# One-hot edge products that read `pre` rows in place: 64-row single-pass products, two blocks at once, in a graph network kernel

## The chip, the cores and the metric

The kernel runs on one core of one Trainium2 chip. The metric is the device time of one execution in microseconds (us), the median of several runs. TensorE (PE) multiplies matrices and writes PSUM, VectorE (DVE) and ScalarE (ACT) work on elements, GpSimd (POOL) issues the indirect transfers here, and SyncE (SP) the plain ones. PEld is TensorE's loading of the stationary operand.

## What is computed

64 graphs of 256 nodes with 256 features pass through four layers. One adjacency matrix `adj` (256 x 256, few entries besides the diagonal) serves all graphs. Layers 0, 1 and 3 are edge networks, layer 2 is an attention.

```python
def edge_layer(h_t, A_a, A_m, W1, b1, W2, b2, Wa, ba, Wm, bm, beta1, beta2, beta3):
    pre_u = jnp.einsum('bud,dk->buk', h_t, W1[:d])
    pre_v = jnp.einsum('bvd,dk->bvk', h_t, W1[d:])
    hidden = jax.nn.relu(pre_u[:, :, None, :] + pre_v[:, None, :, :] + b1)
    S = jax.nn.sigmoid(jnp.einsum('buvk,ko->buvo', hidden, W2)[..., 0] + b2[0])
    a_t = jnp.einsum('buv,bud->bvd', S * A_a, h_t)
    m_t = jnp.einsum('uv,bud->bvd', A_m, h_t) * h_t
    return beta1 * h_t + beta2 * (a_t @ Wa + ba) + beta3 * (m_t @ Wm + bm)
```

The attention layer makes features, a softmax over all pairs plus `adj`, and adds the weighted features to its input. `S` is multiplied by `adj`, so a score is only needed where `adj` is not zero: per edge (u, v), the sum of row u of `pre_u` and row v of `pre_v`, a relu and a weighted sum over 256 numbers.

## The kernel before, in words

The adjacency matrix is cut into 16 blocks of 64 source nodes by 64 target nodes, named (k, m, i): sources 64 k to 64 k + 63 of half m (128 nodes), targets 64 i to 64 i + 63. `edges()` (L529), run once, numbers the edges of each block, at most 128 to a block; what is over goes to a list of rest edges (`left`), and the diagonal is treated apart (`own`, L757). For each block it writes a one-hot matrix `pick` (edge of the block by 64 sources and 64 targets), its transpose for spreading scores back (`gu`, `gva`), and for fetched blocks the node numbers `ids_u`, `ids_v`.

Graphs go in pairs (g = 0, 1, side by side in the last dimension, so a row has 512 numbers). Two such pairs are in work at a time, sides "a" and "b". While the scores of one side's layer are taken (`scores`, L700: "heavy"), the other side's next steps run between them (`after` L880, `attention` L425, `before` L646: "light"); `beside` (L911) interleaves them by counts that each light step yields (`STEPS` L45, `beside` L656). Below, one such interleaving is a stage; a period is six stages, and there are 16 periods, 96 stages. Every engine then works through its instructions in order.

- `before` (L646) makes `pu` and `pv` (pre_u and pre_v + b1) for half m and graph g: a product on PE, a copy on ACT, an addition on DVE. When a half is complete, both go as tables to DRAM (L677, SP's queue), and `fetch` (L814) starts the first six indirect transfers (POOL). `rows_u` and `rows_v` (L833, L841) copy rows on ACT into `pre`, where each made block has a 128-row operand: its 64 u rows and its 64 v rows. The last step, `mixed` (L334), multiplies `adj` into h.
- `scores` (L700) gets the edge sums of 16 blocks in two ways. Made blocks (`made`, L764): one fp32 product of 128 rows, `pick` by `pre`, into a PSUM buffer `ga` (L768); further rows of `pre` are copied as it goes (L773). Fetched blocks (`got`, L783): an indirect transfer of table u's rows, then one of table v's rows that adds (`compute_op`, L829). Rest edges take two such transfers as well. Each sum of a block and graph is rated by one DVE instruction (`rated`, L716), relu times `w2row` with an accumulated sum.
- `rated_all` (L740), for m = 0 and m = 1, takes the tanh (`val`) and multiplies `gva` by it into `rm`, four DVE products each. `spread` (L865) puts `rm` back to source rows by one-hot products with `gu`; `early` (L849) does the rest edges (`guo` by `ro`, products of 64 rows) and the diagonal.

Eight blocks are made and eight fetched, but in two of six stages (`more`, L642: side "a" in the last layer, side "b" in the second edge layer, the stages with attention beside them) six are made and ten fetched. In these two stages graph 1's part of `mixed` is put among the made blocks (L781).

The constants that set this, and the made product:

```python
FAST = [(k, 0, i) for k in range(2) for i in (2, 3)] + [(0, 1, i) for i in range(4)]
FETCHED = [(k, 0, i) for k in range(2) for i in (0, 1)] + [(1, 1, i) for i in range(4)]
MORE = FAST[6:]
FETCHES = [(0, 0), (1, 0), (2, 0), (0, 1), (3, 0), (1, 1)]
FETCHES += [(-1, 0), (2, 1), (4, 0), (3, 1), (-1, 1), (5, 0), (6, 0), (4, 1), (7, 0), (5, 1), (6, 1), (7, 1)]
AHEAD = 6
...
mm(out=t, lhsT=pick[:, k, 4 * m + i, :], rhs=pre[:, n], start=True, stop=True)
```

In `FETCHES`, (f, x) is block f's transfer from table u (x = 0) or v (x = 1), and f = -1 the rest edges. [...]

Of the kernel before, what the change touches and what calls it, by code (L numbers as in the profile page):

```python
# [9 lines left out]
FP = mybir.dt.float32  # L10
I32 = mybir.dt.int32
AF = mybir.ActivationFunctionType
ALU = mybir.AluOpType
# [19 lines left out]
FAST = [(k, 0, i) for k in range(2) for i in (2, 3)] + [(0, 1, i) for i in range(4)]  # L33
FETCHED = [(k, 0, i) for k in range(2) for i in (0, 1)] + [(1, 1, i) for i in range(4)]

MORE = FAST[6:]
FIRST = 4

FETCHES = [(0, 0), (1, 0), (2, 0), (0, 1), (3, 0), (1, 1)]
FETCHES += [(-1, 0), (2, 1), (4, 0), (3, 1), (-1, 1), (5, 0), (6, 0), (4, 1), (7, 0), (5, 1), (6, 1), (7, 1)]  # L40
FETCHES_MORE = FETCHES[:-2] + [(8, 0), (6, 1), (9, 0), (7, 1), (8, 1), (9, 1)]
# [60 lines left out]
def adj_seq_kernel(ctx: ExitStack, tc: tile.TileContext, a: dict, out: bass.AP):  # L102
# [18 lines left out]
    def behind(engine):  # L121

        return tc.issue_after(engine.last.ins)

# [158 lines left out]
    def open_pools(stack):  # L283
        pool = lambda name, bufs, **k: stack.enter_context(tc.tile_pool(name=name, bufs=bufs, **k))
        k = dict(fm=pool("fm", 2), wk=pool("wk", 2), one=pool("one", 1))
        k["ps"] = pool("ps", 5, space=bass.MemoryType.PSUM)
        k["ga"] = pool("ga", 3, space=bass.MemoryType.PSUM)
        return k

    def stages(pools):  # L290
# [211 lines left out]
    def few(stack):  # L502
# [10 lines left out]
        gva = one.tile([P, 2, 8, 64], FP, name="gva")  # L513
# [4 lines left out]
        ids_u = one.tile([P, len(FETCHED + MORE)], I32, name="ids_u")  # L518
        ids_v = one.tile([P, len(FETCHED + MORE)], I32, name="ids_v")
# [9 lines left out]
        def edges():  # L529
            scratch = Scratch(*(  # L530
                (one.tile([P, n * 2 * D], FP, tag=tag + "b", name="scratch"), n * 2 * D)
                for tag, n in (("pre", len(FAST)), ("fetched", FIRST))
# [15 lines left out]
            for m in range(2):  # L548
# [6 lines left out]
                for k in range(2):  # L555
# [3 lines left out]
                    )  # L559

# [31 lines left out]
            for k, m in ((0, 0), (1, 0), (1, 1), (0, 1)):  # L592
# [11 lines left out]
                    vector.scalar_tensor_tensor(gva[:, k, ms, :], gv, 0.5, w, ALU.mult, ALU.mult)  # L604
                    here = [b for b in FETCHED + MORE if b[:2] == (k, m)]
                    if here:
                        i, n = here[0][2], len(here)
                        f = (FETCHED + MORE).index(here[0])
                        for b, x, ids in ((P * m + 64 * k, gu[:, k, ms, :], ids_u), (None, gv, ids_v)):
# [6 lines left out]
                            o = ids[:, f : f + n]  # L616
                            if b is None:
                                vector.tensor_tensor(o, r[:, i : i + n], v0[:, i : i + n], ALU.add)
                            else:
                                vector.tensor_scalar(o, r[:, i : i + n], float(b), None, ALU.add)  # L620
# [21 lines left out]
        def more(st, l):  # L642

            return (st["side"], l) in (("a", LAST), ("b", GNN[1]))

        def before(st, l):  # L646
# [4 lines left out]
            pre = one.tile([P, len(FAST), 2 * D], FP, tag="pre" + st["side"], name="pre")  # L651
# [10 lines left out]
            st["pu"], st["pv"], st["pre"] = pu, pv, pre  # L662
# [4 lines left out]
            for m, g in order:  # L667
# [7 lines left out]
                if g == 1:  # L675
                    for rows, x in zip(st["tables"], (pu, pv)):
                        nc.sync.dma_start(out=rows[blk(m)], in_=flat(x)[:, m])  # L677
                    if m == 0:
                        st["fetches"] = list(FETCHES_MORE if more(st, l) else FETCHES)
# [18 lines left out]
            yield from mixed(st, l, later if past else None, (0,) if more(st, l) else (0, 1))  # L698

        def scores(st, l, placed):  # L700
# [8 lines left out]
            pre = st["pre"]  # L709
# [20 lines left out]
            blocks, fast = (FETCHED + MORE, FAST[:6]) if more(st, l) else (FETCHED, FAST)  # L730
            t = one.tile([P, len(FETCHED + MORE) - FIRST, 2, D], FP, tag="fetched", name="fetched")
            st["fetched"] += [t[:, f] for f in range(len(blocks) - FIRST)]
            fetched = st["fetched"]
            fetch(st, len(FETCHES_MORE))
# [5 lines left out]
            def rated_all(cols, m):  # L740
# [22 lines left out]

            def made():  # L764
                for n, (k, m, i) in enumerate(fast):
                    t = ga.tile([P, 2, D], FP, tag="ga", name="ga")
                    with stay(tensor):
                        mm(out=t, lhsT=pick[:, k, 4 * m + i, :], rhs=pre[:, n], start=True, stop=True)  # L768
                    tile_scores(t, k, m, i)
                    if 2 * n + 2 < len(fast):  # L770

                        with tc.issue_after(past[-1]) if past else nullcontext(), tc.issue_after(st["rows"]):
                            rows_u(st, 2 * n + 2, 2, *FAST[2 * n + 2][:2])  # L773
                            if n != 1:
                                rows_v(st, 2 * n + 2, 2, FAST[2 * n + 2][0])
# [4 lines left out]
                    if n == 2 and more(st, l):  # L780
                        yield from mixed(st, l, None, (1,), ga)  # L781

            def got(made):  # L783
                for f, block in enumerate(blocks):
# [47 lines left out]

        def rows_u(st, f, n, k, m):  # L833

            h = halves[k]
            scalar.copy(
                st["pre"][h, f : f + n],
                st["pu"][h, m].rearrange("p g d -> p (g d)").unsqueeze(1).to_broadcast([64, n, 2 * D]),
            )

        def rows_v(st, f, n, k):  # L841

            for n in range(f, f + n):
                i = FAST[n][2]
                scalar.copy(
                    st["pre"][halves[1 - k], n], st["pv"][halves[i % 2], i // 2].rearrange("p g d -> p (g d)")
                )
# [200 lines left out]
```

## Time and profile before

| what | value |
|---|---|
| median of 3 runs | 3455.84 us (3452.6 to 3463.16) |
| span of the profiled execution, first to last instruction | 3442.3 us (its whole time is not listed) |
| mean granted TensorE clock | 0.990 |
| instructions | 48323 |
| indirect transfers, table u / table v | 832 / 832, and 96 / 96 for the rest edges |
| indirect transfers of the queue q0 | 461.49 MB, 65.2% of the DMA engines' time |

The page gives for each engine its busy time and its share of the span; since matmuls overlap in the array, PE's busy share says only that PE has work. A group line names the operation, what it writes and reads, shapes and count, then busy time in all, the mean ns of one, and the engine's idle time before these instructions with what ended it. An fp32 product appears as two records. A few such lines, in that form:

```profile
L827 POOL DMA_INDIRECT fetched<-tablev,ids_v x832 | 1324.7, 1592 | 353.1 <-issue 249.4
L827 POOL DMA_INDIRECT fetched<-tableu,ids_u x832 | 840.9, 1011 | 544.3 <-DMA tableu<-pu 283.9
L79 DVE SCALAR_TENSOR_TENSOR junk<-fetched,L_gnn_w2row 128x256 f32<-128x256 f32 x1664 | 643.6, 420 | 219.9 <-DMA fetched<-tablev,ids_v 218.3
L79 PE MATMUL ps<-L_gnn_w,hT 128*128 128x512 f32 x1536 | 708.1, 598 | 6.1 <-DMA hT<-in_xT_dram 6.1
```

The first two are POOL's indirect transfers, whose 0.98 to 1.6 us are the time POOL spends on issuing one; the third is the rating of fetched blocks, with 218.3 us in which DVE stood for a landing. L79 is the helper that records every instruction of PE, DVE and ACT, so groups are told apart by tiles.

### The profile page before, as it was taken

Reading aid. Unit: us, or ns where it says so; the run is one execution under the profiler, and the core shown is the slowest. Engines: PE = TensorE matmul, PEld = TensorE weight load, DVE = VectorE, ACT = ScalarE, POOL = GpSimd, SP = SyncE. Lnnn points to the kernel's source line nnn. Section 1 sums busy time; section 2 is a strip of 40 time slices with the busy share of each in tenths; the row PEclk is TensorE's granted clock in tenths of the full one; section 3 lists DMA queues with packets and bytes.
Section 4 is the critical chain, followed back from the end, with each engine's and each line's share of the span. In section 5 each row is a group of like instructions: output and inputs, shape, how many; then the busy total and the mean of one; then the engine's idle time right before and its main releaser. Section 6 shows DMA issues by size and latency. Waiting matters only on the chain.

```text
span 3442.3 us, 48323 instructions
## 1 busy us (share of the span) xinstructions
PE 3349.5 (97%) x14200; PEld 2071.0 (60%) x14200; DVE 2650.7 (77%) x10523; ACT 1556.4 (45%) x2833; POOL 2420.7 (70%) x1882
## 2 busy tenths in 40 slices
PE   6999999999999999999999999999999999999998
PEld 3566565666656566565665656656565665656665
DVE  4777787877877777777777878778787787777776
ACT  2444444444444444544444444444444444444452
POOL 3767777777776767677777776777767776776765
PEclk7999999999999999999999999999999999999999
DMA  5778787887878778787787877878787787787875
GB/s 146 161 181 194 167 200 169 192 184 175 202 168 196 174 180 194 170 195 182 184 184 172 198 173 188 186 167 206 169 194 175 177 199 171 191 177 182 192 169 128
DMA packets 289070, 620.81 MB, mean 180 GB/s; under 512 B 39072, under 2 KB 56352, under 8 KB 288800
## 3 DMA queue, kind: packets, MB, share of 16 engines
q0 software_dynamic: 204800, 461.49, 65.2%
q1 hardware_dynamic: 82416, 154.96, 12.9%
q8 instruction: 115, 1.88, 0.2%
q10 hardware_dynamic: 1584, 1.20, 0.1%
q14 instruction: 155, 1.27, 0.1%
HBM read 500.06 MB, written 117.44 MB: 179 GB/s over the span
## 4 chain that ended last, share of the span: by engine, by line
PE 67%; POOL 11%; DMA 9%; issue 7%; DVE 3%; ACT 2%; ACTq 0%; POOLq 0%; DVEq 0%; SPq 0%
PE ps L79 52%; PE ga L79 15%; POOL fetched L827 10%; DMA fetched<-tablev,ids_v 6%; DVE junk L79 1%; DMA tableu<-pu 1%; POOL left L827 1%; ACT pre L79 1%; DMA fetched<-tableu,ids_u 1%; DVE rm L79 1%; ACT val L79 1%; ACT pu L79 0%; DMA h<-in_x_dram 0%; DMA left<-tablev,left_v 0%; DMA hT<-in_xT_dram 0%
## 5 line engine op out<-in xcount | busy, mean ns | idle before, releaser
L827 POOL DMA_INDIRECT fetched<-tablev,ids_v x832 | 1324.7, 1592 | 353.1 <-issue 249.4
L827 POOL DMA_INDIRECT fetched<-tableu,ids_u x832 | 840.9, 1011 | 544.3 <-DMA tableu<-pu 283.9
L79 DVE SCALAR_TENSOR_TENSOR junk<-fetched,L_gnn_w2row 128x256 f32<-128x256 f32 x1664 | 643.6, 420 | 219.9 <-DMA fetched<-tablev,ids_v 218.3
L79 PE MATMUL ga<-pre,pick 128*128 128x512 f32 x1408 | 728.2, 611 | 24.8 <-ACT pre L79 13.5
L79 PE MATMUL ps<-L_gnn_w,hT 128*128 128x512 f32 x1536 | 708.1, 598 | 6.1 <-DMA hT<-in_xT_dram 6.1
L79 DVE SCALAR_TENSOR_TENSOR junk<-ga,L_gnn_w2row 128x256 f32<-128x256 f32 x1408 | 536.8, 419 | 124.0 <-PE ga L79 121.4
L79 PEld LDWEIGHTS ps<-L_gnn_w,hT 128*128 128x128 f32 x1536 | 280.3, 191 | 324.5 <-issue 294.2
L79 ACT COPY pre<-pv 64x512 f32<-64x512 f32 x704 | 434.2, 617 | 68.1 <-DVE pv L79 56.7
L79 ACT COPY pre<-pu 64x1024 f32<-64x1024 f32 x352 | 361.5, 1044 | 6.6
L79 PE MATMUL ps<-sa,h 128*128 128x256 f32 x1536 | 359.4, 380 | 0.0
L79 PEld LDWEIGHTS ps<-sa,h 128*128 128x128 f32 x1536 | 292.9, 191 | 108.3 <-issue 60.6
L79 ACT COPY pu<-ps 128x256 f32<-128x256 f32 x384 | 143.0, 372 | 470.8 <-PE ps L79 467.8
L79 PEld LDWEIGHTS ga<-pre,pick 128*128 128x128 f32 x1408 | 250.5, 192 | 170.1 <-issue 103.2
L79 DVE TENSOR_TENSOR rm<-gva,val 128x256 f32<-128x256 f32 x768 | 277.7, 420 | 60.8 <-ACT val L79 58.7
L79 PE MATMUL ps<-adj,h 128*128 128x256 f32 x1280 | 293.9, 381 | 3.4 <-issue 3.4
L79 PEld LDWEIGHTS ps<-adj,h 128*128 128x128 f32 x1280 | 244.1, 191 | 78.0 <-issue 41.4
L79 ACT ACTIVATE hb<-hT,L_gnn_zbias,scas 128x512 f32<-128x512 f32 x128 | 97.3, 806 | 414.5 <-DVE hT L79 391.1
L79 PEld LDWEIGHTS ps<-rm,gu 128*64 128x64 f32 x3072 | 176.2, 138 | 131.9 <-issue 70.8
L79 ACT COPY aT<-ps 128x512 f32<-128x512 f32 x192 | 112.5, 586 | 302.6 <-PE ps L79 302.6
L79 PE MATMUL ps<-rm,gu 128*64 128x128 f32 x3072 | 213.8, 281 | 35.5 <-DVE rm L79 35.5
L79 DVE TENSOR_TENSOR pv<-ps,L_gnn_b1row 128x256 f32<-128x256 f32 x384 | 161.9, 422 | 110.2 <-ACT pu L79 101.4
L79 PE MATMUL ps<-mT,L_gnn_Wm 128*128 128x512 f32 x512 | 240.6, 592 | 0.0
(149 smaller groups left out, 4213.1 us busy)
## 6 DMA issues: line engine op xcount, KB each, us to landing
tableu<-pu SPq DMA_DIRECT2D x192, 256.0 KB, 3.8
tablev<-pv SPq DMA_DIRECT2D x192, 256.0 KB, 2.7
hT<-in_xT_dram SPq DMA_DIRECT2D x32, 512.0 KB, 5.1
h<-in_x_dram SPq DMA_DIRECT2D x64, 256.0 KB, 4.8
out_dram<-h SPq DMA_DIRECT2D x64, 256.0 KB, 4.1
fetched<-tableu,ids_u POOLq DMA_INDIRECT x832, 3.8
fetched<-tablev,ids_v POOLq DMA_INDIRECT x832, 5.1
L_gnn_w<-in_L_gnn_W_dram SPq DMA_DIRECT2D x6, 256.0 KB, 4.8
```

The costliest lines, as they stand in the source:

```text
L79: self.last = getattr(self.engine, op)(*a, **k)
L827: this = nc.gpsimd.indirect_dma_start(out=to, out_offset=None, in_=rows, in_offset=bass.IndirectOffsetOnAxis(ap=ids, axis=0), compute_op=( ...
```

## The change

- `pick` by `pre` is replaced. `pre`, `rows_u` and `rows_v` are gone. `pu` and `pv` of each half are split into a high part in the type float32r (a copy on ACT) and the rest (a subtraction on DVE), and the products read these `parts` where they lie. One-hot matrices in float32r, `pick_u` and `pick_v`, are copied once in `edges()`.
- Made blocks come in pairs, k = 0 and k = 1, whose source rows and target rows lie in the same 64 partitions each. A pair is eight products of 64 rows (v rest, u rest, u high, v high; for each, k = 1 and k = 0), into two `ga` buffers, issued one behind another. `FAST` and `FETCHED` are chosen anew for that.
- All stages have 8 made and 8 fetched blocks; `more`, `MORE` and `FETCHES_MORE` are gone, and `mixed` is whole again at the end of `before`.
- Blocks 4 and 5 of the fetched are read from table v first, and u is added (`V_FIRST`); a transfer reads only half 0's table where it can.
- `rm` is one product of 128x1024 for each m, with `gva` and `rm` laid out anew.
- PSUM: four buffers for `ps` and four for `ga`.

```diff
-FAST = [(k, 0, i) for k in range(2) for i in (2, 3)] + [(0, 1, i) for i in range(4)]
-FETCHED = [(k, 0, i) for k in range(2) for i in (0, 1)] + [(1, 1, i) for i in range(4)]
-
-MORE = FAST[6:]
+FAST = [(k, m, 2 * j + k) for m in range(2) for j in range(2) for k in range(2)]
+FETCHED = [(k, m, 2 * j + 1 - k) for m in range(2) for j in range(2) for k in range(2)]
+
 FIRST = 4
+
+
+V_FIRST = (4, 5)
 
 FETCHES = [(0, 0), (1, 0), (2, 0), (0, 1), (3, 0), (1, 1)]
 FETCHES += [(-1, 0), (2, 1), (4, 0), (3, 1), (-1, 1), (5, 0), (6, 0), (4, 1), (7, 0), (5, 1), (6, 1), (7, 1)]
-FETCHES_MORE = FETCHES[:-2] + [(8, 0), (6, 1), (9, 0), (7, 1), (8, 1), (9, 1)]
...
+    def soon():
+
+        return tc.high_priority(offset=1000)
...
-        k["ps"] = pool("ps", 5, space=bass.MemoryType.PSUM)
-        k["ga"] = pool("ga", 3, space=bass.MemoryType.PSUM)
+        k["ps"] = pool("ps", 4, space=bass.MemoryType.PSUM)
+        k["ga"] = pool("ga", 4, space=bass.MemoryType.PSUM)
...
-        def mixed(st, l, later=None, graphs=(0, 1), buffers=None):
-
-            if 0 in graphs:
-                st["mT"] = one.tile([P, 2, 2, N], FP, tag="mT" + st["side"], name="mT")
-            mT = st["mT"]
-            for g in graphs:
-                t = buffers.tile([P, 2, 256], FP, tag="ga", name="ga") if buffers else psum()
-                for m in range(2):
-                    if buffers and m == 1:
-                        yield
-                    for c in range(2):
-                        mm(out=t[:, m, :], lhsT=st["h"][g][:, c, blk(m)], rhs=adj[:, c, :], start=c == 0, stop=c == 1)
+        def mixed(st, l, later=None):
+
+            st["mT"] = mT = one.tile([P, 2, 2, N], FP, tag="mT" + st["side"], name="mT")
+            for g in range(2):
+                t = psum()
+                product(t, st["h"][g], adj)
...
-        gva = one.tile([P, 2, 8, 64], FP, name="gva")
+        gva = one.tile([P, 2, 2, 4, 64], FP, name="gva")
+
+
+        pick_u = one.tile([P, 2, 2, P], FR, name="pick_u")
+        pick_v = one.tile([P, 2, 2, P], FR, name="pick_v")
...
+                for k, h in enumerate(halves):
+                    mine = slice(4 * m + k, 4 * m + k + 3, 2)
+                    scalar.copy(pick_u[h, m], pick[h, k, mine, :])
+                    scalar.copy(pick_v[h, m], pick[halves[1 - k], k, mine, :])
...
-            pre = one.tile([P, len(FAST), 2 * D], FP, tag="pre" + st["side"], name="pre")
+            parts = {
+                x: [one.tile([P, 2, 2 * D], FR, tag=x + y + st["side"], name=x + y) for y in "hl"] for x in "uv"
+            }
...
-                    if m == 0:
-                        rows_u(st, 0, 2, 0, 0)
-                    rows_v(st, 4 - 4 * m, 2, 0)
-                    st["rows"] = scalar.last.ins
+
+                    for x, (high, low) in ((pu, parts["u"]), (pv, parts["v"])):
+                        scalar.copy(high[:, m], flat(x)[:, m])
+                        vector.tensor_tensor(low[:, m], flat(x)[:, m], high[:, m], ALU.subtract)
...
-            yield from mixed(st, l, later if past else None, (0,) if more(st, l) else (0, 1))
+            yield from mixed(st, l, later if past else None)
...
-                for g in range(2):
-                    for k in range(2):
-                        ms = slice(4 * m, 4 * m + 4)
-                        i = BLOCKS + 16 * m + 8 * g + 4 * k
-                        vector.tensor_tensor(
-                            rm[:, k, ms, g, :], gva[:, k, ms, :],
-                            val[:, i : i + 4].unsqueeze(2).to_broadcast([P, 4, 64]), ALU.mult
-                        )
+                of = slice(BLOCKS + 16 * m, BLOCKS + 16 * m + 16)
+                vector.tensor_tensor(
+                    rm[:, m], gva[:, m].rearrange("p k i v -> p (k i) v").unsqueeze(2).to_broadcast([P, 8, 2, 64]),
+                    val[:, of].rearrange("p (g x) -> p x g", g=2).unsqueeze(3).to_broadcast([P, 8, 2, 64]), ALU.mult
+                )
...
+            def sums(m, j):
+
+
+                both_ = [ga.tile([P, 2, D], FP, tag="ga", name="ga") for _ in halves]
+                order = [(pick_v, "v", 1, j), (pick_u, "u", 1, m), (pick_u, "u", 0, m), (pick_v, "v", 0, j)]
+                for n, (pick_, x, part, block) in enumerate(order):
+                    for k in (1, 0):
+                        h, first = halves[k], (n, k) == (0, 1)
+                        with stay(tensor) if first else behind(tensor), nullcontext() if first else soon():
+                            mm(out=both_[k], lhsT=pick_[h, m, j, :], rhs=st["parts"][x][part][h, block],
+                               start=n == 0, stop=n == 3)
+                return both_
+
             def made():
-                for n, (k, m, i) in enumerate(fast):
-                    t = ga.tile([P, 2, D], FP, tag="ga", name="ga")
-                    with stay(tensor):
-                        mm(out=t, lhsT=pick[:, k, 4 * m + i, :], rhs=pre[:, n], start=True, stop=True)
-                    tile_scores(t, k, m, i)
-                    if 2 * n + 2 < len(fast):
-
-                        with tc.issue_after(past[-1]) if past else nullcontext(), tc.issue_after(st["rows"]):
-                            rows_u(st, 2 * n + 2, 2, *FAST[2 * n + 2][:2])
-                            if n != 1:
-                                rows_v(st, 2 * n + 2, 2, FAST[2 * n + 2][0])
+                for n, (k, m, i) in enumerate(FAST):
+                    if k == 0:
+                        pair = sums(m, i // 2)
+                    tile_scores(pair[k], k, m, i)
                     if n in (1, 2) and not diagonal_later:
                         itself(n - 1)
                     count.append(n)
                     yield
-                    if n == 2 and more(st, l):
-                        yield from mixed(st, l, None, (1,), ga)
...
-                rows = st["tables"][x]
+                y = 1 - x if f in V_FIRST else x
+                rows, ids = st["tables"][y], (ids_u, ids_v)[y]
                 if f < 0:
                     to, ids = st["left"], (left_u, left_v)[x]
                     rows = rows.rearrange("n (g d) -> (n g) d", g=2)
                 else:
-                    to, ids = st["fetched"][f].rearrange("p g d -> p (g d)"), (ids_u, ids_v)[x][:, f : f + 1]
-                    if f < FIRST:
+                    k, m, i = FETCHED[f]
+                    to, ids = st["fetched"][f].rearrange("p g d -> p (g d)"), ids[:, f : f + 1]
+                    if (m, i // 2)[y] == 0:
                         rows = rows[blk(0)]
...
```

More of the change, by code (lines that the diff above doesn't have):

```diff
@@ L10 @@
 FP = mybir.dt.float32
+FR = mybir.dt.float32r
 I32 = mybir.dt.int32
@@ L517, in few @@
         gvo = one.tile([P, N], FP, name="gvo")
-        ids_u = one.tile([P, len(FETCHED + MORE)], I32, name="ids_u")
-        ids_v = one.tile([P, len(FETCHED + MORE)], I32, name="ids_v")
+        ids_u = one.tile([P, len(FETCHED)], I32, name="ids_u")
+        ids_v = one.tile([P, len(FETCHED)], I32, name="ids_v")
         left_u = one.tile([P, 1], I32, name="left_u")
@@ L530, in edges @@
             scratch = Scratch(*(
-                (one.tile([P, n * 2 * D], FP, tag=tag + "b", name="scratch"), n * 2 * D)
-                for tag, n in (("pre", len(FAST)), ("fetched", FIRST))
+                (one.tile([P, n * 2 * D], FP, tag=tag, name="scratch"), n * 2 * D)
+                for tag, n in (("fetchedb", FIRST), ("fetched", len(FETCHED) - FIRST))
             ))
@@ L603, in edges @@
                     scalar.copy(gv, t[:, :, halves[1 - k]])
-                    vector.scalar_tensor_tensor(gva[:, k, ms, :], gv, 0.5, w, ALU.mult, ALU.mult)
-                    here = [b for b in FETCHED + MORE if b[:2] == (k, m)]
+                    vector.scalar_tensor_tensor(gva[:, m, k], gv, 0.5, w, ALU.mult, ALU.mult)
+                    here = [b for b in FETCHED if b[:2] == (k, m)]
                     if here:
-                        i, n = here[0][2], len(here)
-                        f = (FETCHED + MORE).index(here[0])
+                        i = slice(here[0][2], here[0][2] + 3, 2)
+                        f = FETCHED.index(here[0])
+                        f = slice(f, f + 3, 2)
                         for b, x, ids in ((P * m + 64 * k, gu[:, k, ms, :], ids_u), (None, gv, ids_v)):
@@ L615, in edges @@
                             vector.tensor_reduce(r, y, AX.X, ALU.add)
-                            o = ids[:, f : f + n]
+                            o = ids[:, f]
                             if b is None:
-                                vector.tensor_tensor(o, r[:, i : i + n], v0[:, i : i + n], ALU.add)
+                                vector.tensor_tensor(o, r[:, i], v0[:, i], ALU.add)
                             else:
-                                vector.tensor_scalar(o, r[:, i : i + n], float(b), None, ALU.add)
+                                vector.tensor_scalar(o, r[:, i], float(b), None, ALU.add)
             t = psum().rearrange("p a (b e) -> p (a b) e", e=P)
@@ L640, in few @@
         flat = lambda t: t.rearrange("p m g d -> p m (g d)")
-        def more(st, l):
-            return (st["side"], l) in (("a", LAST), ("b", GNN[1]))
         def before(st, l):
@@ L660, in before @@
             ]
-            st["pu"], st["pv"], st["pre"] = pu, pv, pre
+            st["pu"], st["pv"], st["parts"] = pu, pv, parts
             if l != GNN[1]:
@@ L678, in before @@
                     if m == 0:
-                        st["fetches"] = list(FETCHES_MORE if more(st, l) else FETCHES)
+                        st["fetches"] = list(FETCHES)
                         if numbered:
@@ L708, in scores @@
             diagonal_later = placed and (st["side"], l) in (("b", GNN[0]), ("a", GNN[1]))
-            pre = st["pre"]
             raw = wk.tile([P, LATE.stop], FP, tag="raw", name="raw")
@@ L729, in scores @@
             st["left"] = left = one.tile([P, D], FP, tag="left", name="left")
-            blocks, fast = (FETCHED + MORE, FAST[:6]) if more(st, l) else (FETCHED, FAST)
-            t = one.tile([P, len(FETCHED + MORE) - FIRST, 2, D], FP, tag="fetched", name="fetched")
-            st["fetched"] += [t[:, f] for f in range(len(blocks) - FIRST)]
+            t = one.tile([P, len(FETCHED) - FIRST, 2, D], FP, tag="fetched", name="fetched")
+            st["fetched"] += [t[:, f] for f in range(len(FETCHED) - FIRST)]
             fetched = st["fetched"]
-            fetch(st, len(FETCHES_MORE))
+            fetch(st, len(FETCHES))
             def tile_scores(t, k, m, i):
@@ L779, in made @@
                     yield
-                    if n == 2 and more(st, l):
-                        yield from mixed(st, l, None, (1,), ga)
             def got(made):
-                for f, block in enumerate(blocks):
+                for f, block in enumerate(FETCHED):
                     if f == FIRST:
@@ L831, in fetch @@
                 fetches.append(this.ins)
[L833 to L847, printed above, removed]
         def early(st):
@@ L871, in spread @@
                     for k, h in enumerate(halves):
-                        mm(out=t[h, :, quarter(i)], lhsT=gu[:, k, 4 * m + i, :], rhs=rm[:, k, 4 * m + i],
+                        mm(out=t[h, :, quarter(i)], lhsT=gu[:, k, 4 * m + i, :], rhs=rm[:, m, 4 * k + i],
                            start=True, stop=True)
```

## The prediction

> **What bounds the kernel now.** I read the page's busy rows first, then the chain that ended last, then the groups by form, then windows over one period, then the timelines of PE and POOL. All durations are of the one profiled execution, whose span is 3442.3 us; the page gives no other time of it. The median of the runs is 3455.84, so about 13.5 us lie around the span; I add that to every span below.
>
> ```profile
> PE 3349.5 (97%) x14200; PEld 2071.0 (60%) x14200; DVE 2650.7 (77%) x10523; ACT 1556.4 (45%) x2833; POOL 2420.7 (70%) x1882
> ...
> PE 67%; POOL 11%; DMA 9%; issue 7%; DVE 3%; ACT 2%; ACTq 0%; POOLq 0%; DVEq 0%; SPq 0%
> ```
>
> PE is the first bound, but not alone: some 27% of the chain is POOL, DMA landing and "issue", the fetches. Next, what one period of six stages costs (a stage is one layer's scores of one side beside the other side's light steps; its end is the second tanh on `val`). Columns: length, then busy time of PE, PEld, DVE, ACT, POOL.
>
> ```profile
> 1421.42:1460.58 39.16, 38.28 (x162) 23.84 (x158) 30.98 (x123) 18.28 (x37) 26.89 (x22) 1.00 0.77 167
> 1460.58:1501.37 40.79, 40.40 (x178) 25.10 (x177) 32.71 (x128) 17.96 (x37) 28.62 (x23) 1.00 0.81 187
> 1501.37:1534.93 33.56, 33.56 (x148) 22.29 (x146) 26.86 (x106) 14.38 (x26) 25.94 (x21) 1.00 0.89 215
> 1534.93:1565.53 30.60, 30.00 (x133) 19.99 (x133) 24.51 (x100) 14.77 (x26) 23.06 (x18) 1.00 0.86 202
> 1565.53:1596.79 31.26, 31.26 (x128) 17.90 (x127) 23.18 (x96) 15.72 (x27) 22.07 (x17) 1.00 0.75 163
> 1596.79:1628.50 31.71, 31.71 (x128) 17.71 (x126) 25.21 (x100) 15.75 (x28) 21.77 (x17) 1.00 0.78 178
> ```
>
> Stages 1 and 2 carry the attention and 6 made / 10 fetched blocks; 3 to 6 have 8 / 8. The POOL column hides its load: between two transfers it has 0.30 us of "issue". The POOL timeline:
>
> ```profile
> 1558.59 1.54 POOL L827 DMA_INDIRECT fetched<-tablev,ids_v  x1 [0.30 <-issue]
> 1560.44 0.99 POOL L827 DMA_INDIRECT fetched<-tableu,ids_u  x1 [0.30 <-issue]
> ...
> 1594.32 0.98 POOL L827 DMA_INDIRECT fetched<-tableu,ids_u  x1 [4.05 <-DMA tableu<-pu]
> ```
>
> An 8-fetch stage issues 18 transfers: 9 x (0.98 + 0.30) + 9 x (1.55 + 0.30) = 28.2 us, of 30.6 to 33.6. So stages 3 to 6 have two bounds close together: PE, and the loop table write, 18 fetches, last landing (about 5.4 us), rating, `val`, `rm`, the other side's light steps, next table write.
>
> **The change part by part.** Groups that it removes or grows, and how TensorE treats 64-row products:
>
> ```profile
> L79 PE MATMUL ga<-pre,pick 128*128 128x512 f32 x1408 | 728.2, 611 | 24.8 <-ACT pre L79 13.5
> L79 ACT COPY pre<-pv 64x512 f32<-64x512 f32 x704 | 434.2, 617 | 68.1 <-DVE pv L79 56.7
> L79 ACT COPY pre<-pu 64x1024 f32<-64x1024 f32 x352 | 361.5, 1044 | 6.6
> L79 DVE TENSOR_TENSOR rm<-gva,val 128x256 f32<-128x256 f32 x768 | 277.7, 420 | 60.8 <-ACT val L79 58.7
> ```
>
> ```profile
> 1524.25 1.02 PE L79 MATMUL ga<-pre,pick 128*128 128x512 f32 x2
> 1525.20 1.13 PE L79 MATMUL ps<-ro,guo 64*128 64x256 f32 x8
> 1526.27 1.12 PE L79 MATMUL ga<-pre,pick 128*128 128x512 f32 x2
> 1527.23 3.17 PE L79 MATMUL ps<-L_gnn_w,hT 128*128 128x512 f32 x7
> ```
>
> *PE, removed.* A made product is two records; among others of its kind they start 0.86 us apart in all (0.43 each for 512 columns). There are 1408/2 = 704: 704 x 0.862 = 607 us.
>
> *PE, added.* 96 stages x 4 pairs = 384 pairs, each eight single-record products of 64 rows and 512 columns. Two prices are needed.
>
> First, one pass. No row shows a reduced-precision product. [...]
>
> Second, two row halves at once. The row of `ro,guo` shows it: eight records of 64x256, each 0.2135 of stream, start to next start in 1526.27 - 1525.20 = 1.07 us, where one after another would be 1.71. So halves overlap. [...] I take 1.25, since that group is the same shape of work with the same neighbours. The eight weight loads are inside that price (the `ro,guo` group hides eight too).
> 384 x 1.25 = 480: PE saves 607 - 480 = 127 us, 1.9 us in each 8-made stage (6.9 to 5.0), 0.17 in stages 1 and 2 (5.17 to 5.0; they now make 8). [...]
>
> *ACT.* Removed 704 x 0.617 + 352 x 1.044 = 802 us. Added: 384 copies of 128x512, nearest the 64x512 row: 384 x 0.617 = 237. ACT is no bound; what counts is that `pu` of the second half has 2 x 0.62 us before it, not 1.04 + 1.24, so its table goes out up to 1 us sooner, and that PE's waits for `pre` (13.5 on PE, 31.0 on weight loads) end. Of that 44.5 I count 20 as path.
>
> *DVE.* Added: 384 subtractions 128x512; the SBUF-only `own<-pu,pv` of that shape takes 689 ns: 265 us. The four `rm` products of a stage half (1.43 us together in the timeline) become one of 128x1024 (1.21, the setup's row of that shape): 192 x 0.22 = 42 less. Net +222, 2.3 us a stage: 2873 busy. Hidden while DVE's 5 to 8 us of waiting per stage is for PE and DMA; if that cover is gone it is +222. Behind the subtractions of half 0 in DVE's queue stand `pv` of half 1 (1.4 us later) and so `tablev`, for which POOL's eighth transfer waits; the seven before it (some 10 us) cover that.
>
> *POOL and DMA queue.* 64 blocks fewer: 64 x (1.59 + 1.01 + 0.60) = 205 us, all in stages 1 and 2, where PE leads: worth nothing by itself. Stages 3 to 6 keep 18 transfers and 28.2 us. The v-first order of two blocks and whole-table reads of two others stay behind transfers that wait for the same tables: nothing. SP's queue is unchanged.
>
> *Moved.* Graph 1's mix (8 records x 0.2135 = 1.72 us PE, one multiply on DVE) leaves the score steps of stages 1 and 2 for the end of the light steps one stage earlier: stage 2 loses 1.72 us before its table write, stage 6 gains 1.72 behind it, stage 1 both. No DMA is in it.
>
> *PSUM, new waits.* Four `ps` buffers for five: 0 to 1 us a stage (weight loads of `ps` wait for DVE's `junk` 30.9 us in all today); I take 0 for the sum. PE's products now wait for the rest parts from DVE; they are made before the last scores and the mix (3.4 us of PE) of the stage before: hidden; uncovered 0.62 + 0.69 = 1.3 us a stage, 126 in all. Queued behind PE's wait would be everything on PE. Setup: eight small copies, +3.
>
> *Sum.* By PE alone a period saves 4 x 1.9 + 2 x 0.17 = 7.9 us. By the loop: stage 2's table is 1.9 sooner (0.17 + 1.72); stages 3 and 4 are then one unbroken run of POOL (1500.91 to 1560.1), so they stay at -1.9; stage 5's light steps, with about 1.6 us less PE before the table write, make stage 6 end 3.5 sooner; stage 1 adds 0.17. So 3.7 against 7.9, and the smaller wins: 16 x 3.7 = 60. With 20 for `pre` and 3 for the setup: 3442 - 60 - 20 + 3 = 3365, and 13.5 around it: **3378 us**, 3340 to 3420 by itself. What is late next is POOL's queue.
>
> **Rivals.** *PE's full saving* (0.15): the loop has more slack than I count (stage 5's last landing was near 1594, its `val` at 1596.8). 3442 - 127 - 20 + 3 + 13.5 = 3312. [...] For: chain 67% PE. Against: 27% of it is fetches.
>
> *DVE takes over* (0.17, slower): DVE works in order, and its ratings of fetched blocks already hold it 218 us for landings. If the subtractions between `pv` of half 0 and of half 1 push the evacuations that the light steps need (`hT`, `pv`, `sa`), tables go out later, landings too, and DVE stands longer in front of them. All 222 us on the path and PE's 127 + 20 won: 3456 + 222 - 147 = 3531. It decides from where DVE's busy share of stages 3 to 6 passes about 0.93. Against: now 0.74 to 0.80, and 2.3 us makes it 0.82 to 0.9.
>
> *The products don't stream as said* (0.13, slower): 2.11 a pair, +203 - 20: about 3640. For: no row shows them. Against: `ro,guo`.
>
> *The fetch loop holds everything* (0.07): stages 3 to 6 keep their length, stages 1 and 2 win under 0.5 us: within 0.3%, 3450.
>
> **How the numbers follow.** Forecast 0.48. About 0.3% (10 us) is what a measurement of this kernel can tell from no change. Faster: 0.48 and 0.15, less 0.03 for a forecast eaten by the `ps` buffers: 0.60. Same: 0.07 and 0.01: 0.08. Slower: 0.17, 0.13 and 0.02: 0.32. The range takes in the PE rival nearly to its floor and the DVE rival: 3250 to 3535; it leaves out the product rival and the floor's tail.
>
> **What would show it.** PE: a group of eight 64*128 records of 64x512, start to next start near 1.25 us; 0.9 or 2.1 would be the ends. ACT near 990 us, DVE near 2870, POOL near 2250. Stages 3 and 4 should show POOL without waits for `tableu`, and PE with gaps for `rm` or `sa`. Wrong if PE's share stays at 97% with a shorter span (rival one), or if waits of PE for DVE grow to 100 us or more (rival two).

## The result, and the profile after

The changed kernel took **3585.86 us** (median of 4, 3577.73 to 3588.51) against 3454.98 before (4 runs): a ratio of 1.0372, 95% interval 1.0348 to 1.0397. It is 131 us slower; the forecast was 78 faster. The time lies above the range.

The page's busy row and chain (the chain was followed only a few per cent back, so it says nothing here):

```profile
PE 3286.3 (92%) x15864; PEld 2102.0 (59%) x15864; DVE 2827.9 (79%) x10331; ACT 995.2 (28%) x2169; POOL 2304.3 (64%) x1754
...
PE 4%; DVE 1%; DMA 1%; POOL 0%; ACT 0%; issue 0%; POOLq 0%; DVEq 0%; ACTq 0%
```

The span is 3576.0. PE is busy 63.2 us less, and idle 289.7 instead of 92.8: the span grew by 196.9 - 63.2 = 133.7. The mean granted clock fell from 0.990 to 0.969, which is 0.031 x 3576 - 0.010 x 3442 = 76 us of full clock, partly within PE's idle time. So PE's work shrank by 63 to 140 us (predicted: 127), and PE now stands idle.

One period, cut like that of the prediction (the same six stages, second tanh to second tanh; PE, PEld, DVE, ACT, POOL, clock):

```profile
1478.67:1512.16 33.49, 29.37 (x135) 19.14 (x132) 25.85 (x106) 10.70 (x25) 19.92 (x15) 0.90 0.64 121
1512.16:1561.13 48.97, 46.04 (x212) 28.79 (x212) 36.18 (x130) 14.92 (x34) 23.04 (x18) 0.97 0.59 140
1561.13:1602.11 40.98, 39.00 (x206) 26.30 (x202) 34.12 (x116) 9.74 (x22) 28.05 (x21) 1.00 0.78 195
1602.11:1634.63 32.52, 30.34 (x152) 21.22 (x152) 26.45 (x98) 8.13 (x18) 25.09 (x18) 0.95 0.84 189
1634.63:1666.78 32.15, 29.95 (x140) 17.58 (x142) 24.89 (x94) 9.09 (x20) 24.58 (x18) 1.00 0.77 174
1666.78:1699.35 32.57, 30.35 (x152) 17.85 (x148) 27.49 (x99) 8.99 (x19) 25.06 (x19) 1.00 0.81 177
```

In each of these stages PE is idle 2 to 4 us in all; in those of the prediction it was 0 to 0.9. A stage's tanh no longer falls at the same point of the attention, so I use another cut below: from one write of table u's second half to the next. By it the six stages of a period, A to F, take on the mean, in us (14 periods; the attention runs beside E and F):

| kernel | A | B | C | D | E | F | sum |
|---|---|---|---|---|---|---|---|
| before | 30.0 | 33.5 | 31.7 | 31.7 | 41.9 | 40.8 | 209.7 |
| after | 29.2 | 34.4 | 31.8 | 33.2 | 45.5 | 43.8 | 217.9 |

16 x 8.2 = 131: the loss is there every period, and 6.6 of the 8.2 lie in E and F (stages 1 and 2 of the prediction, by this cut). There PE is busy on the mean as long as before (41.3 and 40.5 us; before 41.7 and 40.0), but idle 4.2 and 3.4 us instead of 0.2 and 0.8. Of this idle time, 3.3 and 2.0 us are waits for `logits` and `e` from ACT, the steps of the softmax.

The groups that answer to those shown of before, first PE's `rm` group of before for comparison, then PE's made products (start, length):

```profile
L79 PE MATMUL ps<-rm,gu 128*64 128x128 f32 x3072 | 213.8, 281 | 35.5 <-DVE rm L79 35.5
```

```profile
L81 DVE TENSOR_TENSOR rm<-gva,val 128x1024 f32<-128x1024 f32 x192 | 234.9, 1224 | 54.1 <-ACT val L81 54.1
L81 DVE TENSOR_TENSOR ul<-pu,uh 128x512 fp32r<-128x512 f32 x192 | 132.0, 687 | 5.8 <-ACT uh L81 5.5
L81 DVE TENSOR_TENSOR vl<-pv,vh 128x512 fp32r<-128x512 f32 x192 | 131.4, 685 | 0.4
L81 PE MATMUL ps<-rm,gu 128*64 128x128 f32 x3072 | 213.7, 287 | 103.6 <-DVE rm L81 103.1
L835 POOL DMA_INDIRECT fetched<-tableu,ids_u x768 | 926.2, 1206 | 790.6 <-DMA tableu<-pu 553.7 <-issue 211.0 <-DVE ids_u L81 15.6
```

```profile
1524.04 0.49 PE L81 MATMUL ga<-vl,pick_v 64*128 64x512 f32 x2
1524.38 0.39 PE L81 MATMUL ga<-ul,pick_u 64*128 64x512 f32 x2
1524.60 0.40 PE L81 MATMUL ga<-uh,pick_u 64*128 64x512 f32 x2
1524.84 0.40 PE L81 MATMUL ga<-vh,pick_v 64*128 64x512 f32 x2
1525.17 1.97 PE L81 MATMUL ps<-rm,gu 128*64 128x128 f32 x32
```

A pair takes 1525.17 - 1524.04 = 1.13 us from start to next start, the median of all 384. PE waits 103.1 us for `rm` (35.5 before). That `rm` is now made in one product is not the reason: in stage B, where PE waits longest, it starts 1.38 us after `rm` does, before 1.24. POOL waits 553.7 us for `tableu` (283.9), nearly all of it at the starts of F and A. One such start of F, before and after:

```profile
1460.10 0.98 POOL L827 DMA_INDIRECT fetched<-tableu,ids_u  x1 [4.87 <-DMA tableu<-pu]
```

```profile
1522.14 1.16 POOL L835 DMA_INDIRECT fetched<-tableu,ids_u  x1 [19.28 <-DMA tableu<-pu]
```

On the mean it waits 18.8 us at F and 15.0 at A (before 5.6 and 5.2). The last transfer of E and of F goes out 27.9 and 29.8 us after the write that opens the stage, sooner than before (35.9 and 36.2, with 22 transfers for 18), but the next write comes only after 45.5 and 43.8 us. So in E and F the fetches do not hold the loop: the light steps, attention among them, bring the next tables late.

### The profile page after: what moved, and what is told of

Same layout as the page of the kernel before. It is cut to its first block, busy times and chain, and to the rows that moved or that the text cites. A ratio compares the mean times of both kernels' runs of the same rounds, so it can differ in the third digit from the quotient of the medians.

```text
span 3576.0 us, 49956 instructions
## 1 busy us (share of the span) xinstructions
PE 3286.3 (92%) x15864; PEld 2102.0 (59%) x15864; DVE 2827.9 (79%) x10331; ACT 995.2 (28%) x2169; POOL 2304.3 (64%) x1754
## 3 DMA queue, kind: packets, MB, share of 16 engines
q1 hardware_dynamic: 82416, 154.96, 12.5%
## 5 line engine op out<-in xcount | busy, mean ns | idle before, releaser
L835 POOL DMA_INDIRECT fetched<-tableu,ids_u x768 | 926.2, 1206 | 790.6 <-DMA tableu<-pu 553.7
L835 POOL DMA_INDIRECT fetched<-tablev,ids_v x768 | 1122.7, 1462 | 351.4 <-issue 227.7
L81 DVE SCALAR_TENSOR_TENSOR junk<-fetched,L_gnn_w2row 128x256 f32<-128x256 f32 x1536 | 593.9, 421 | 250.0 <-DMA fetched<-tablev,ids_v 231.5
L81 DVE SCALAR_TENSOR_TENSOR junk<-ga,L_gnn_w2row 128x256 f32<-128x256 f32 x1536 | 586.3, 419 | 149.6 <-PE ga L81 148.4
L81 PE MATMUL ps<-adj,h 128*128 128x256 f32 x1536 | 351.4, 382 | 6.0 <-issue 5.8
L81 PE MATMUL ps<-rm,gu 128*64 128x128 f32 x3072 | 213.7, 287 | 103.6 <-DVE rm L81 103.1
L81 DVE TENSOR_TENSOR rm<-gva,val 128x1024 f32<-128x1024 f32 x192 | 234.9, 1224 | 54.1 <-ACT val L81 54.1
L81 PE MATMUL ps<-aT,L_gnn_Wa 128*128 128x512 f32 x512 | 240.6, 592 | 0.0
L81 PE MATMUL ga<-vl,pick_v 64*128 64x512 f32 x768 | 198.6, 510 | 27.7 <-DVE junk L81 14.1
L81 PE MATMUL ps<-f,logits 128*128 128x258 f32 x512 | 158.0, 445 | 45.9 <-ACT logits L81 44.4
L835 POOL DMA_INDIRECT left<-tablev,left_v x96 | 152.4, 1587 | 29.9 <-issue 27.8
```

Of the source, the lines that this page charges most:

```text
L81: self.last = getattr(self.engine, op)(*a, **k)
L835: this = nc.gpsimd.indirect_dma_start(out=to, out_offset=None, in_=rows, in_offset=bass.IndirectOffsetOnAxis(ap=ids, axis=0), compute_op=( ...
```

## The experiments

Theory one: the made pairs are issued at the wrong place. `stay` does nothing in the attention stages, so the pairs run early, and PE stands idle between the softmax steps. (In before it does nothing there either, yet the products stand between the steps, as the lines below show.) Theory two: the four added subtractions are not hidden on DVE. Rivals: the balance of 8 made and 8 fetched, the PSUM split, and the product itself. Each kernel was timed beside the kernel before on the same chip (3451 to 3463 us there), so ratios are compared.

### The place of the pairs

**a_stay**: after, with each pair's first product held at its place.

```diff
-with stay(tensor) if first else behind(tensor), nullcontext() if first else soon():
+with behind(tensor), nullcontext() if first else soon():
```

> The changed kernel with one word different: the first product of every pair is tied behind the last PE instruction written before it, also in the stages with attention beside them, so that two of the four pairs stand between the softmax's steps again and don't run ahead. Hoisting theory (the pairs ran ahead of their place, the softmax chain lost its cover, PE idles there and its clock is halved for about 7 us): the chain is covered, the granted clock goes from 0.97 to 0.985 or more, 40 to 80 us are won (3505 to 3545). DVE theory (the subtractions stand in the way of evacuations): no gain, within 15 us of 3586. Imbalance theory (8 fetched for 10 leaves POOL idle, then late): little, 0 to 20 us.

3512.59, ratio 1.0168 (1.0149 to 1.0186). **a_stay2**, the same kernel on another chip: 3531.77, ratio 1.0201 (1.017 to 1.0233).

> The first made product of every pair held at its place, as in a_stay, run once more beside the next kernel. 3513 in its first run: 3505 to 3520 if the two series can be compared. In the second series DVE and ACT stood up to 3 us for PE although the records of the products had ended (a_nosub: 97 such waits of PE for sa, 109 us); a_stay had none. If those belong to the series, a_stay2 shows them too and takes 3540 to 3600.

So the early issue costs 0.017 to 0.020 of 3455, 59 to 70 us, about half of the loss. By stage (A to F) a_stay takes 29.6, 33.0, 32.9, 31.5, 44.7 and 42.4: A to D together are as long as before (127.0 and 126.9), and all that is left of the loss, 4.4 us a period, lies in E and F. PE in one attention, in before, after and a_stay:

```profile
1441.10 0.44 PE L79 MATMUL ps<-ident,e 128*128 128x128 f32 x2
1441.37 1.46 PE L79 MATMUL ga<-adj,h 128*128 128x256 f32 x6
1442.67 1.02 PE L79 MATMUL ga<-pre,pick 128*128 128x512 f32 x2
1443.53 0.60 PE L79 MATMUL ps<-ident,e 128*128 128x128 f32 x4
1443.96 1.02 PE L79 MATMUL ga<-pre,pick 128*128 128x512 f32 x2
1444.86 2.01 PE L79 MATMUL ps<-f,logits 128*128 128x258 f32 x8
```

```profile
1499.75 0.44 PE L81 MATMUL ps<-ident,e 128*128 128x128 f32 x2 [0.33 <-ACT logits L81]
1501.77 1.30 PE L81 MATMUL ps<-ident,e 128*128 128x128 f32 x4 [1.57 <-ACT e L81]
1503.80 3.81 PE L81 MATMUL ps<-f,logits 128*128 128x258 f32 x8 [0.73 <-ACT logits L81]
```

```profile
1471.77 0.33 PE L81 MATMUL ps<-ident,e 128*128 128x128 f32 x1 [0.66 <-DVE e L81]
1472.03 0.50 PE L81 MATMUL ga<-vl,pick_v 64*128 64x512 f32 x2
...
1473.43 0.94 PE L81 MATMUL ps<-ident,e 128*128 128x128 f32 x4 [0.20 <-ACT e L81]
1474.30 0.50 PE L81 MATMUL ga<-vl,pick_v 64*128 64x512 f32 x2
...
1475.43 2.01 PE L81 MATMUL ps<-f,logits 128*128 128x258 f32 x8
```

After has no pair from 1495.3 to 1524.0. Eight records `ps<-f,logits` then take 3.81 us; in before, and in a_stay with pairs between the steps, they take 2.01. The windows of after show why, in the clock's column behind the five engines:

```profile
1498.00:1500.00 2.00, 1.67 (x10) 1.13 (x8) 1.94 (x10) 1.65 (x5) 1.69 (x2) 1.00 0.69 172
1500.00:1502.00 2.00, 0.42 (x3) 0.15 (x1) 2.00 (x9) 1.85 (x5) 1.70 (x2) 0.96 0.89 134
1502.00:1504.00 2.00, 1.27 (x5) 0.70 (x5) 2.00 (x12) 0.95 (x3) 0.86 (x1) 0.50 0.97 132
1504.00:1506.00 2.00, 2.00 (x5) 1.63 (x6) 0.55 (x5) 1.48 (x5) 0.00 (x0) 0.50 0.72 114
```

Ahead of this halving PE's longest gap is 1.57 us, and the clock stays at 0.50 for 6.8 us; PE had only 0.42 us of work in a stretch of 2 us. It is no exception: ahead of 18 of the 35 halvings of this trace no gap within 8 us was over 2.0 us, and ahead of all 35 PE was busy at most 0.68 of the last 4 us. Keeping each gap short was not enough here. How thin the work must be is not shown.

**a_fill**: after, with useless 128x256 products in that chain instead (4 at its head, then 1 a step).

> The changed kernel with useless products put between the softmax's steps (six 128x256 fp32 products per attention, 2.6 us of PE, 82 us in all): PE work is only added. Hoisting theory: clock back to 0.985 or more, the two attention stages 2 to 4 us shorter each, so 30 to 100 us faster in spite of the added work. DVE or imbalance theory: as slow or up to 82 us slower.

3575.46, ratio 1.0353 (1.0336 to 1.037): the clock rose to 0.982, but the filling added 44 us of busy time on PE. The time is that of after within the intervals, so the clock's share is not shown apart.

### The subtractions on DVE

**b_subs**: before, with four subtractions a stage that nobody reads, where the change has them. **b_late**: the two of half 0 written behind half 1's `pv`.

```diff
+low = one.tile([P, 2 * D], mybir.dt.bfloat16, tag="low", name="low")
+for i in range(2):
+    vector.tensor_tensor(low, flat(pu)[:, m], flat(pv)[:, m], ALU.subtract)
```

> The kernel before with four more DVE subtractions of 128x512 a stage at the place where the change has its own (their result is not read): 264 us of DVE work added and nothing else. DVE theory: 80 to 200 us slower. Hoisting and imbalance theory: under 40 us slower.

> b_subs (before with four useless subtractions a stage) with those of half 0 moved behind half 1's pv. Theory one, place: of the 96 us that they cost in b_subs less than half is left, 3465 to 3500. Theory two, volume: 3540 to 3555 as in b_subs.

b_subs: 3547.31, ratio 1.0275 (1.0257 to 1.0292). b_late: 3549.72, ratio 1.0258 (1.0229 to 1.0287). 264 us of DVE work cost 89 to 95 us (by the ratios). b_late is in effect b_subs once more: in 94 of 96 stages of its trace two subtractions still run ahead of the last `pv`, so it tests no other place. By stage, 5.8 of the 6.4 us that b_subs loses in a period lie in E and F. **b_hole** and **b_hole2** put the four behind the additions to `sa` at a stage's start; in stages E and F of before, DVE is busy 4 to 66% from 8 to 14 us after the table write, and 87 to 100% from 24 to 38 us (slices of 2 us, mean of 14 periods). In the trace of b_hole2 the four run 5.4 to 12.5 us after the write.

```diff
 it = vector.tensor_tensor(sa[:, m], sa[:, m], t, ALU.add)
+for i in range(4):
+    with behind(vector):
+        vector.tensor_tensor(low, sa[:, i // 2], sa[:, 1 - i // 2], ALU.subtract)
```

> Before with the four useless subtractions a stage of b_subs, but issued behind the additions to sa at a stage's start instead of beside the last pv. In b_subs the time from the last transfer to val grew by 1.6 to 3.8 us (before 5.0 to 6.8), since the subtractions stand in DVE's queue ahead of the last ratings of the stage before. Theory one, that place: DVE has 8 to 14 us after the table write with 15 to 60% busy, so they cost little there, 3455 to 3490. Theory two, DVE's volume: 3540 to 3555 wherever they stand.

> b_hole with sa as the operand of the four useless subtractions, so that the load of the next hT has nothing to wait for. b_hole lost 6.7 and 2.0 us in the two stages around that load and 0.2 to 0.4 in the four others. Theory one, place (ahead of the last ratings, or in DVE's open stretch): 3460 to 3500. Theory two, volume: 3540 or more.

b_hole read `hT` where b_hole2 reads `sa`: 3603.13, ratio 1.0434 (1.0396 to 1.0471). Its loss is my own operand's, since the next load of `hT` had to wait for its readers:

```profile
L79 PE MATMUL ps<-L_gnn_w,hT 128*128 128x512 f32 x1536 | 750.1, 628 | 112.4 <-DMA hT<-in_xT_dram 112.4
```

b_hole2: 3475.95, ratio 1.0039 (1.0026 to 1.0053). The same DVE work costs 13 us there instead of 89 to 95. DVE in the same stage's end of b_subs, and after it in b_hole2:

```profile
1547.15 0.42 DVE L79 TENSOR_TENSOR pv<-ps,L_gnn_b1row 128x256 f32<-128x256 f32 x1
1547.61 0.42 DVE L79 TENSOR_TENSOR own<-ps,pv 128x256 f32<-128x256 f32 x1
1547.95 1.41 DVE L79 TENSOR_TENSOR low<-pu,pv 128x512 bf16<-128x512 f32 x2
1549.28 0.42 DVE L79 TENSOR_TENSOR pv<-ps,L_gnn_b1row 128x256 f32<-128x256 f32 x1
1549.86 0.43 DVE L79 TENSOR_TENSOR rm<-gva,val 128x256 f32<-128x256 f32 x1 [0.16 <-ACT val L79]
```

```profile
1516.42 0.69 DVE L79 TENSOR_TENSOR sa<-sa,ps 128x512 f32<-128x512 f32 x1 [1.51 <-PE ga L79]
1517.03 0.68 DVE L79 TENSOR_TENSOR mT<-ps,hT 128x512 f32<-128x512 f32 x1
1517.63 0.68 DVE L79 TENSOR_TENSOR low<-sa 128x512 bf16<-128x512 f32 x1
```

In b_subs the work stands in front of the last `pv` (so of table v) and of `rm`, with no gap on DVE before it; in b_hole2 it stands where DVE had just waited 1.51 us. The mean time from a stage's last transfer to its tanh goes the same way (A to F): before 5.3, 5.7, 6.8, 5.4, 5.9, 5.0; b_subs 6.6, 7.3, 9.2, 8.0, 7.9, 8.8; b_hole2 5.4, 5.8, 6.2, 5.7, 6.0, 5.2. It grows in every stage of b_subs, though only E and F get much longer.

### The smaller parts

**b_88**: before with 8 made and 8 fetched blocks in all stages (`more` returns False). **b_ps4**: before with four buffers for `ps`, four for `ga`. **b_e**: before with the attention's 128x128 additions to `e` on ACT.

> The kernel before with 8 made and 8 fetched blocks in all stages and the mix whole at the end of the light steps; products, copies and buffers as before. PE gets 64 products more (55 us), POOL 128 transfers fewer. Imbalance theory: slower by 90 us or more, POOL's waits for table u near 500 us as in the changed kernel. Hoisting theory: only the added PE work and a little cover lost, 20 to 60 us slower, clock 0.985 or more. DVE theory: at most the 55 us of PE.

> Before with four PSUM buffers for ps and four for ga instead of five and three. Put at nothing in the prediction (0 to 1 us a stage): 3450 to 3475; if the buffer counts, up to 3550.

> Before with the attention's 128x128 additions to e on ACT instead of DVE (0.2 us each, 8 in each attention stage, 1.6 us). If DVE's load in the attention stages binds before too, 3430 to 3445; if PE does (97% busy), within 8 of before.

b_88: 3471.99, ratio 1.0054 (1.0037 to 1.0071), 19 us. b_ps4: 3476.9, ratio 1.0038 (1.0026 to 1.005), 13 us. b_e: 3460.62, ratio 1.0004 (0.9987 to 1.0021): 33 us of DVE work less, and nothing gained. **a_more**, a_stay with 6 made and 10 fetched in the attention stages and graph 1's mix among the made blocks again: 3521.3, ratio 1.0156 (1.0123 to 1.0189), no better than a_stay. **a_stay_e**, a_stay with the additions to `e` on ACT: 3533.24, ratio 1.0188 (1.0156 to 1.022), no gain either.

> The kernel with the pairs held in place, and again six made and ten fetched blocks and graph 1's mix among the made ones in the two stages with attention. The 8/8 step cost the kernel before 20 us, by PE work that the pairs do more cheaply: 0 to 30 us faster than 3513. If the attention stages are bound by PE's idle gaps between softmax steps, the mix fills them: 30 to 60 us faster.

> The kernel with the pairs held in place, and the four 128x128 additions an attention makes for its logits on ACT, not on DVE: 44 us of DVE work less, all in the two stages with attention. DVE theory with its place in those stages: 20 to 60 us faster than 3513. If DVE's load counts evenly over all stages: about 16 us (0.36 of the work, as 96 of 264). If ACT's longer way counts: 0 or slower.

### What didn't fit: leaving the work out of the kernel after

All of these start from a_stay; a_nosub, a_keep and a_high leave the rest parts out of the sums. **a_nosub** drops the subtractions and reads the high part twice, **a_keep** makes them and doesn't read them, **a_high** drops them with the four products that read them, **a_late** writes those of half 0 where b_late does (in its trace one of the two runs behind the last `pv` in 32 stages, and the order is that of a_stay in 62), and **a_hole** moves all four, and the first pair, behind the spreading.

```diff
-vector.tensor_tensor(low[:, m], flat(x)[:, m], high[:, m], ALU.subtract)
```

> The kernel with the pairs held in place, without the DVE subtractions: its eight products a pair stay, but read the high part twice, so the rest part is left out of the computation. DVE theory: the subtractions cost here what they cost alone (96 us), so 3400 to 3430, faster than the kernel before, since PE's own saving of some 130 to 160 us then shows. If the subtractions were covered in this kernel: within 25 us of 3513.

> a_nosub once more (the rest parts are left out: no subtractions, and the products with the rest read the high part a second time), beside a_stay2. Theory one, the stalls belong to the kernel's order: again near 3593. Theory two, they belong to the series: 3400 to 3450, some 70 to 100 under a_stay2, since the subtractions alone cost 96 in b_subs.

> a_stay with the subtractions made but not read: the products read the high part twice (the rest parts are left out of the result), so DVE's work is that of a_stay and PE's order and waits are those of a_nosub. If a_nosub's slowness comes from its PE side (the spreading's end came 82 and 106 us later in all than its records say, in a_stay 4 and 26), a_keep has it too: 3590 to 3680. If it comes from anything on DVE: 3510 to 3540.

> As the one without subtractions, and with only the four products of the high parts a pair; the rest part is left out of the computation. PE streams 164 us less than with eight. If PE is still the bound once DVE is relieved: 80 to 150 us under the run without subtractions. If the loop of fetches and landings or DVE is the bound: under 40 us below it.

> a_stay with the subtractions of half 0 moved behind half 1's pv, so that all four stand together after the last pv. Nothing is left out. Theory one, their place in DVE's queue: half 1's pv and the table come up to 1.4 us sooner in each stage: 3430 to 3490. Theory two, DVE's volume in the stage: within 12 of a_stay2.

> a_stay with the subtractions taken to the first made step of their own stage, behind the additions to sa, and that step behind the spreading. Nothing is left out. Theory one (place): the time from the last transfer to val falls back by 1.5 to 3 us a stage and the pairs lie later between the softmax steps: 3420 to 3480, so it may beat both kernels. Theory two (volume): 3505 to 3535 as a_stay.

| kernel | us | ratio to before (interval) |
|---|---|---|
| a_nosub | 3593.2 | 1.0379 (1.0338 to 1.042) |
| a_nosub2 (same) | 3576.35 | 1.0339 (1.0312 to 1.0367) |
| a_keep | 3530.98 | 1.0203 (1.0183 to 1.0223) |
| a_high | 3562.83 | 1.0296 (1.0265 to 1.0326) |
| a_late | 3527.71 | 1.0192 (1.0163 to 1.0221) |
| a_hole | 3539.86 | 1.024 (1.021 to 1.0269) |

Theory two let me expect 3400 to 3450 for a_nosub. It is slower than a_stay, twice, and a_keep, with the same order on PE, is as fast as a_stay. a_hole, whose trace has the subtractions 7.6 to 12.2 us after the write, gains nothing either. So nothing here shows that DVE's 264 us bind in the kernel after. But a_nosub is no clean test: without the subtractions 534 of DVE's other 9947 instructions stand at another place than in a_keep. In A, B, C and E additions to `sa` come behind more ratings of `ga`; in F, where a_nosub2 loses most to a_keep (46.4 and 43.4 us), the order is the same. In a_nosub PE waits longer for `sa`, which a_keep shows much less; a_nosub2 first, then a_keep:

```profile
L81 PE MATMUL ps<-sa,h 128*128 128x256 f32 x1536 | 403.0, 414 | 82.9 <-DVE sa L81 76.4 <-issue 6.3
```

```profile
L81 PE MATMUL ps<-sa,h 128*128 128x256 f32 x1536 | 381.5, 398 | 30.1 <-DVE sa L81 28.1 <-issue 1.9
```

Those additions to `sa` waited in turn for `ps<-rm,gu`: early in F and in A, DVE stood 0.8 to 2.0 us for it after the end in its records (means of two places each, both runs; a_keep 0.2 to 0.6). a_stay2 has 0.1 to 0.5 of it and a_stay, the same kernel, none, so it does not come from the kernel alone. I found no cause, and b_hole2 and b_ps4 have some of it too. (In these traces, and all but those of before, after, a_stay, a_fill, b_88 and b_subs, about one in six of PE's semaphore events is missing, so some waits read "issue" or "remote".) a_high has the least PE work and the lowest clock, 0.956 (a_nosub 0.969, a_nosub2 0.975, a_stay 0.977). It fits the clock's part of theory one, but wasn't tested by itself.

## Why the prediction was wrong, point by point

- *A pair at 1.25 us*: right in kind. Start to next start is 1.13, but the 1.25 took in what the products before and after a group lose. They lose it here too: next to a pair, records of 512 columns start 0.52 and 0.53 us apart instead of 0.43 (medians), so the like price is 1.129 + 0.094 + 0.104 = 1.33. Around `ro,guo` in the trace of before they start 0.52 and 0.53 us apart too, and that group takes 1.064: 1.26 in all, close to the 1.25. The runs show the size of these losses, not their cause. The 1.25 (as the 0.9 and 2.1 beside it, and the floor that the range names) also takes 0.2135 us for a product of 64 rows and 512 columns; no run shows a product at this pace, it was my estimate. In its place after has a pair's products start in twos, one in each row half: the second two 0.34 us after the first, then two every 0.23 us (medians). So the product rival is out.
- *PE saves 127 us*: about right. By that price it is 607 - 384 x 1.33 = 96, by busy time and clock 63 to 140. **The failed step came next**: that this, with the moved mix, shortens the loop by 3.7 us a period, stages 1 and 2 by 0.17 and 1.9. The period grew by 8.2 us, E and F by 3.6 and 3.0, and there PE stood 6.6 us more in all. The sum had no term for what the products did between the softmax steps; a_stay shows this to be about half of the loss. What makes the other half in the kernel after stays open.
- *DVE's 222 us hidden behind 5 to 8 us of waiting a stage*: wrong for the place where the change puts them, as far as the kernel before shows it. I took idle time from anywhere in the stage as cover. In E and F it lies 8 to 14 us after the table write, and the subtractions stand around the last `pv`, ahead of ratings and `rm`. In the kernel before this costs 89 to 95 us, and 13 in the open stretch, shown by b_subs against b_hole2. In the kernel after, its share isn't shown, since neither leaving the work out nor moving it gained anything.
- *The cover of `tablev` by seven transfers*: it held; the eighth transfer waits in no stage of after. The fourth waits for the landing of its own block's rows of u: in stage D it starts 5.4 us after the first, before 4.4, and POOL needs 30.9 us for the 18 transfers instead of 29.0.
- *Products moved out of the attention at no cost* (the mix, six blocks' rows): wrong, and no rival had it. I asked what was removed from these stages, not what kept PE supplied between the softmax steps. The pairs' early issue is visible in the diff (`stay` for the first product, `soon` for the others). It costs 59 to 70 us; the clock's part of that is not shown apart.
- *8 / 8 in the attention stages at a gain of 0.17 us each*: not tested. b_88 lost 19 us, but it makes the two added blocks by the old product, 64 x 0.86 = 55 us of PE work. *PSUM at nothing*: 13 us lost when done alone to before.
- *ACT 990, DVE 2870, POOL 2250 us busy*: 995, 2828, 2304, right; of no help, as they don't set the end.
- *13.5 us around the span*: misread. In the listed runs the time is 1.7 us longer than the span; the profiled execution of before was simply faster than those. It does not bear on the sign.
- *Rival two* (0.17) named the right sign, and one of its marks came, PE's wait for DVE above 100 us (103.1 for `rm`). Its other mark did not: DVE's busy share of A to D is 0.79 to 0.83, not 0.93. Its price of 222 was too high, it had no part for the order on PE, and its mechanism is shown in the kernel before only.

The account in the terms of the runs: 59 to 70 for the place of the pairs; in the kernel before 89 to 95 for the subtractions, 19 for the balance and 13 for PSUM. Together 180 to 197, against 131. These may not be added: three were measured in the kernel before, one of them with the old product, and in the kernel after a_nosub and a_hole gained nothing. So what the new product gains by itself is not shown. What is open is the half of the loss that a_stay keeps, all in E and F, and why leaving the subtractions out makes the changed kernel slower. The order of fetches (`V_FIRST`) and the choice of blocks were not tested by themselves. No version beat the kernel before: b_e is equal to it, and a_more and a_stay are the best with the new products.

## What to carry to other kernels

Cover has a place: before calling work on an in-order engine hidden, find the idle stretch, and see what is queued between it and the new work. A product off the critical chain may be what keeps PE supplied and its clock up in another engine's chain (here a mean clock of 0.969 in after, 0.977 in a_stay and 0.982 in a_fill); when it is replaced or moved, look at what then stands between the steps of that chain. And when the bound engine gets work taken away, ask stage by stage what sets the pace then: in E and F the last fetch went out 8 and 6 us sooner, and the stages still grew.

## What the hardware showed unexpectedly

- A granted clock of 0.50 for 6.8 us after a thin stretch without any PE gap over 1.57 us.
- Two products of 64x512 in different row halves, one record each, start 3 ns apart, the next two 0.34 us later, then two every 0.23 us (medians in after), and a group of eight takes 1.13, with the loading of eight weights inside; the records of 512 columns before and after it lose 0.09 and 0.10.
- A subtraction of 128x512 took 685 to 687 ns with a float32r result (after) and 683 with a bf16 result (b_hole2): no more than 4 ns between them.
